# Turning round the order of the states and within-chunk matmuls in a state-space and feed-forward layer

## The chip, the cores and the metric

The kernel runs on one core of one Trainium2 chip. Times are microseconds (us) of device time. The engines are TensorE (PE in the profile; its weight loads are PEld), VectorE (DVE), ScalarE (ACT), GpSimd (POOL) and SyncE (SP, which only issues DMAs here). PE writes into PSUM, of which the kernel uses eight banks; the other engines read the results out of it.

## What is computed

The reference is one layer on x of shape (4, 512, 256): a state-space block and then a feed-forward block, each with a normalization before it and a gate behind it. The state-space block has 32 heads of width 8 with a state of 64:

```python
h = _layernorm(x) * (1 + ca) + sa
proj = h @ W_in.T                                  # xBC, z, A_log
xBC = causal_conv_of_4(xBC) + conv_b               # x, Bm, Cm
a = -softplus(A_log);  Lm = exp(segsum(a))
M = einsum('blhn,bshn,bhls->bhls', Cm, Bm, Lm)
y = einsum('bhls,bshp->blhp', M, x) + D * x
x = x + ga * ((y * silu(z + z_bias)) @ W_out.T)
h = _layernorm(x) * (1 + cb) + sb
x = x + gb * (fwht(silu(h @ W1.T) * (h @ W3.T)) @ W2.T)
```

## The kernel before, in words

The 512 tokens of a batch entry are cut into NC = 8 chunks of Q = 64. Within a chunk, M is formed directly ("products within chunks"). Between chunks, a state is carried: each chunk's own contribution to the state ("states"), a scan over the chunks, and the product of C with the carried state.

The heads are worked on in 8 units n = (half of the heads, batch entry), each of two groups m = 2n and 2n + 1 (pp = m % 2), and each group of four pairs of heads k = 4m + g, g = 0 to 3. So k runs from 0 to 63 and m from 0 to 15. For one k:

- `project` (called twice) makes B and C: six matmuls each (line 251, tiles pbc and pcc, one of three PSUM buffers), then the convolution in `conv`, two instructions on ACT (lines 387 and 389), two on DVE (390, 391), one on POOL (392).
- `prep_l` makes the decays l of that k (PE line 428, tile pl; an exponential on ACT, line 430).
- `attend`, called for every odd k, multiplies C and B chunk by chunk for k - 1 and k into two PSUM tiles pG (line 262). These matmuls have an order written out by hand, in a chain: in each chunk k first, then k - 1. Then DVE multiplies each pG into its l (line 458, one instruction of 128x512 each). That product is what the within-chunk matmuls read.
- `turn_b` transposes B (PE line 464, tile bT) and ACT copies it to SBUF as bt (line 466).

For one group m of four k:

- `states` (line 530): 16 matmuls ps, for t = 0 to 3 (pairs of chunks) and g = 0 to 3, from bt of that g and from xwz of that t. g picks one of four column strips of PE, 32 columns wide. ACT then copies ps out to st (line 535).
- `intra` (line 546): 32 matmuls py, for chunk c = 0 to 7 and g = 0 to 3, from l of that g and from xpad of that chunk, in the same four strips. The two groups of a unit add into the same PSUM tile, so the first matmul of the even group starts the sum.
- `turn_states` (sT, line 557, a scan on DVE in line 559, POOL in 563) and `inter` (pi, line 572) carry the state on.

xpad and xwz are made once per unit, in `x_part3`: for each half hf of the tokens four transposes (line 513), then on DVE one instruction for xpad of chunks 4 hf to 4 hf + 3 (line 517) and two for xwz of t = 2 hf and 2 hf + 1 (line 520). The even group of a unit comes just behind it; the odd group finds both halves long done. bt and l come in the order of k, so those of g = 3 and g = 2 are the latest of a group.

What sets the order: each piece of work has a due time, k plus an offset or 4m + 4 plus an offset, and is traced in the order of these times (an agenda, lines 780 on). A planner of the framework then places the instructions on the five engines: it simulates a timeline and takes, on each engine, the earliest-traced instruction that is ready, and allots PSUM and SBUF buffers on the way. It keeps data dependencies; `issue_after` (the helper `behind` in this kernel) adds an order between two instructions of one engine. In the finished program each engine works its own queue in order. PSUM has three buffers for the projections (tag p), three for everything else of this part (tag m: pl, pG, bT, ps, sT, xt, po) and one each for py and pi.

After the scan, from about 445 us on, the feed-forward block runs (tiles f, pdy, pdyi); its first matmuls are mixed with the last groups of the scan.

Of the kernel before, what the change touches and what calls it, by code (L numbers as in the profile page):

```python
# [17 lines left out]
ALU = mybir.AluOpType  # L18
# [6 lines left out]
NC = S // Q  # L25
# [5 lines left out]
def mamba_ffn(tc, ctx, u, c_t, wmod, win_t, cw, cb, zb, dsk, wo_t, w13_t, w2_t,  # L31
              k_ident, k_reset, k_dl, k_dr, k_had, k_own, out):
    nc = tc.nc
    ve, ac, gp, pe = nc.vector, nc.scalar, nc.gpsimd, nc.tensor
# [25 lines left out]
    def work(shape, name, tag, bufs=2, dtype=F32):  # L60
        return wk.tile(shape, dtype, name=name, tag=tag, bufs=bufs)

    def mtile(shape, name):
        return ps_m.tile(shape, F32, name=name, tag="m")
# [18 lines left out]
    last = {}  # L83

    def behind(*engines):
        stack = ExitStack()
        for e in engines:
            stack.enter_context(tc.issue_after(last[e].ins))
        return stack
# [322 lines left out]
    lts, bcs, ccs, bts, exs, des, xcs, xds, dcs, stt, pys, zts = ({} for _ in range(12))  # L412
# [29 lines left out]
    def attend(k):  # L442


        ks = (k - 1, k)
        pgs = [mtile([128, S], f"pG{n}") for n in ks]
        chain = Chain()
        for c in range(NC):


            for n, pg in list(zip(ks, pgs))[::-1]:
                for j in range(2):
                    i, o = 64 * j, 64 * (j ^ (n % 2))
                    r, l = slice(i, i + 64), slice(Q * c, Q * c + Q)
                    chain.matmul(pg[o : o + 64, l], bcs[n][r, l], ccs[n][r, l], start=True, stop=True,
                                 tile_position=(i, o))
        for n, pg in zip(ks, pgs):
            ve.tensor_tensor(lts[n], pg, lts[n], ALU.mult)  # L458

    def turn_b(k):  # L460
        bc = bcs[k]
# [63 lines left out]
    def states(m):  # L525
        pp = m % 2
        pst = mtile([128, 4, 128], f"ps{m}")
        for t in range(4):
            for g in range(4):
                pe.matmul(pst[32 * g : 32 * g + 32, t], xwz[:, t, 4 * g + 2 * pp : 4 * g + 2 * pp + 2].rearrange("p h q x -> p (h q x)"),  # L530
                          bts[4 * m + g][:, t], start=True, stop=True, tile_position=(0, 32 * g))
        for g in range(4):
            bts.pop(4 * m + g)
        stt[m] = work([128, 4, 128], f"st{m}", "st", 1)
        ac.activation(stt[m], pst, AF.Copy)

    def intra(m):
        n, pp = divmod(m, 2)
        if pp == 0:
            pys[n] = (ps_1.tile([128, S], F32, name=f"py{n}", tag="y"),  # L540
                      ps_1.tile([128, S], F32, name=f"pi{n}", tag="yi"))
        py = pys[n][0]
        for c in range(NC):
            for g in range(4):
                l = slice(Q * c, Q * c + Q)
                pe.matmul(py[32 * g : 32 * g + 32, l], xpad[:, pp, c, g], lts[4 * m + g][:, l],  # L546
                          start=(pp == 0 and c == 0), stop=(pp == 1), skip_group_check=True,
                          tile_position=(0, 32 * g))
        for g in range(4):
            lts.pop(4 * m + g)  # L550
# [229 lines left out]
    for m in range(16):  # L780
        at_time(4 * m + 4 + T["states"], states, m)
        at_time(4 * m + 4 + T["intra"], intra, m)
        at_time(4 * m + 4 + T["turn"], turn_states, m)
        at_time(4 * m + 4 + T["inter"], inter, m)
        if m:
            at_time(4 * m + T["load_d"], load_d, m)
    for k in range(NP):
        if k % 2:
            at_time(k + T["attend"], attend, k)
        at_time(k + T["turn_b"], turn_b, k)  # L790
        if k >= AHEAD:
            at_time(k + T["proj_b"], project, k, 0)
            at_time(k + T["proj_c"], project, k, 1)
        if k >= LOOK_P:
            at_time(k + T["prep_l"], prep_l, k)
# [112 lines left out]
```

## Time and profile before

| | us |
|---|---|
| three runs | 584.75, 587.55, 587.96 (median 587.55) |
| the profiled execution, whole | 587.68 |
| its span, first to last instruction | 585.9 |
| mean granted TensorE clock | 0.988 of full speed |
| PE busy | 549.5 (94%) |
| DVE busy | 401.7 (69%) |
| ACT busy | 387.2 (66%) |
| POOL busy | 325.8 (56%) |

A row of the timeline has the start in us, the length in us (from the first start to the last end of what is merged in the row), the engine, the line, the operation, written and read tiles, a shape and a count; in brackets, the idle time of the engine just before it and what ended it. A matmul of this kernel with two float32 operands shows as two records, so a group of 16 or 32 matmuls shows as 32 or 64. A row of the waits has the waiting instruction, what it waited for, the total in us, how often, and the longest. A row of groups has the count, the busy time and the mean duration of one instruction:

| PE instruction | records | busy us | mean ns |
|---|---|---|---|
| py, L546 | 1024 | 29.9 | 222 |
| ps, L530 | 512 | 22.1 | 275 |
| pG, L262 | 2048 | 40.7 | 222 |
| pi, L572 | 896 | 16.6 | 227 |

The two instructions on DVE that the change orders are 64 of line 458, 683 ns each.

### The profile page before, as it was taken

How to read it: one execution, taken by the hardware profiler on the slowest of the kernel's cores; microseconds unless marked ns; L12 is line 12 of the kernel's file. 1: busy time of each engine (PE TensorE's matmuls, PEld its weight loads, DVE VectorE, ACT ScalarE, POOL GpSimd, SP SyncE). 2: the span in 40 equal slices, each digit the busy share in tenths (PEclk: the TensorE clock that was granted, in tenths of full speed). 3: DMA queues.
4: the chain of work that ended last, by engine and by line, in shares of the span. 5: the costliest groups of instructions: out<-in, count | busy, mean ns of one | idle time of the engine just before them, and what ended most of it. 6: DMA issues, size and time to landing. Idle time of an engine off the chain costs nothing.

```text
span 585.9 us, 16301 instructions
## 1 busy us (share of the span) xinstructions
PE 549.5 (94%) x6867; PEld 432.6 (74%) x6868; DVE 401.7 (69%) x672; ACT 387.2 (66%) x666; POOL 325.8 (56%) x299
## 2 busy tenths in 40 slices
PE   9868899899899989999999899899989999999996
PEld 5545686667687766877777677677767898888886
DVE  5978667977878675889787779787855454333243
ACT  5988779788966877896794787769584242232321
POOL 5862447435635668466465557477666645334341
PEclk9998999999999989999999899999989999999999
DMA  7351101401232343014103142164157037004021
GB/s 230 106 184 35 49 2 74 66 16 59 67 63 56 117 143 121 2 62 137 42 4 113 75 112 104 61 170 149 38 156 286 2 127 217 35 1 152 1 82 36
DMA packets 41793, 51.99 MB, mean 89 GB/s; under 512 B 17943, under 2 KB 29941, under 8 KB 41721
## 3 DMA queue, kind: packets, MB, share of 16 engines
q1 hardware_dynamic: 41448, 50.96, 28.5%
q8 instruction: 54, 0.88, 0.6%
q14 instruction: 19, 0.15, 0.1%
q10 hardware_dynamic: 272, 0.00, 0.0%
HBM read 33.51 MB, written 17.44 MB: 87 GB/s over the span
## 4 chain that ended last, share of the span: by engine, by line
PE 40%; DVE 5%; ACT 4%; POOL 2%; issue 1%; DMA 1%; POOLq 0%; DVEq 0%
PE f L251 15%; PE pcc L251 4%; PE pdy L724 4%; PE pdyi L724 4%; PE pbc L251 3%; PE po L610 2%; PE pG L262 1%; PE py L546 1%; PE bT L464 1%; ACT xn L281 1%; PE ps L530 1%; PE pi L572 1%; DVE cc L390 1%; DVE bc L390 1%; PE pt L291 1%
## 5 line engine op out<-in xcount | busy, mean ns | idle before, releaser
L392 POOL TENSOR_TENSOR bc<-bc,cv 128x509 f32<-128x509 f32 x64 | 69.6, 1088 | 55.8 <-DVE bc L391 37.9
L251 PE MATMUL f<-h,wf 128*128 128x512 f32 x384 | 97.7, 395 | 0.0
L392 POOL TENSOR_TENSOR cc<-cc,cv 128x509 f32<-128x509 f32 x64 | 69.7, 1090 | 50.1 <-DVE cc L391 39.1
L251 PEld LDWEIGHTS f<-h,wf 128*128 128x128 f32 x384 | 69.2, 190 | 12.5
L717 POOL TENSOR_TENSOR fl<-ft,fh 128x512 fp32r<-128x512 f32 x31 | 40.0, 1293 | 57.8 <-ACT fh L716 55.1
L390 DVE SCALAR_TENSOR_TENSOR cc<-pcc,cw_sb,cc 128x511 f32<-128x511 f32 x64 | 47.6, 743 | 32.2 <-ACT cv L389 32.1
L387 ACT ACTIVATE cc<-pcc,cb_sb,cw_sb 128x512 f32<-128x512 f32 x64 | 50.2, 784 | 22.8 <-PE pcc L251 17.3
L251 PE MATMUL pcc<-ht,wq 128*128 128x512 f32 x192 | 55.8, 424 | 6.1 <-DVE bc L391 6.1
L387 ACT ACTIVATE bc<-pbc,cb_sb,cw_sb 128x512 f32<-128x512 f32 x64 | 50.1, 782 | 15.4 <-PE pG L262 14.0
L716 ACT ACTIVATE fh<-ft 128x512 fp32r<-128x512 f32 x32 | 20.2, 631 | 57.6 <-DVE ft L713 27.7
L712 DVE SCALAR_TENSOR_TENSOR ft<-ft,f 128x512 f32<-128x512 f32 x32 | 21.9, 688 | 52.4 <-ACT ft L711 52.3
L251 PE MATMUL pcc<-hr,wq 128*128 128x512 f32 x192 | 54.5, 417 | 2.9 <-DVE bc L391 2.2
L390 DVE SCALAR_TENSOR_TENSOR bc<-pbc,cw_sb,bc 128x511 f32<-128x511 f32 x64 | 47.6, 744 | 11.1 <-ACT cv L389 10.8
L251 PE MATMUL pbc<-hr,wq 128*128 128x512 f32 x192 | 52.4, 406 | 1.4 <-DVE cc L391 1.0
L251 PE MATMUL pbc<-ht,wq 128*128 128x512 f32 x192 | 51.7, 402 | 1.6 <-DVE bc L391 1.6
L251 PEld LDWEIGHTS pcc<-ht,wq 128*128 128x128 f32 x192 | 35.7, 196 | 19.1 <-DVE bc L391 7.0
L391 DVE SCALAR_TENSOR_TENSOR bc<-pbc,cw_sb,bc 128x510 f32<-128x510 f32 x64 | 47.5, 743 | 1.2
L391 DVE SCALAR_TENSOR_TENSOR cc<-pcc,cw_sb,cc 128x510 f32<-128x510 f32 x64 | 47.6, 743 | 1.0
L458 DVE TENSOR_TENSOR l<-pG,l 128x512 f32<-128x512 f32 x64 | 41.2, 683 | 8.3 <-PE pG L262 7.9
L464 PE MATMUL bT<-ident,bc 128*128 128x128 f32 x256 | 41.2, 283 | 4.6 <-ACT bt L466 2.4
L466 ACT ACTIVATE bt<-bT 128x512 f32<-128x512 f32 x64 | 38.8, 606 | 9.8 <-PE bT L464 9.5
L262 PEld LDWEIGHTS pG<-cc,bc 64*64 64x64 f32 x2048 | 34.8, 134 | 13.7 <-issue 9.7
(154 smaller groups left out, 1244.8 us busy)
## 6 DMA issues: line engine op xcount, KB each, us to landing
wq<-win_t SPq DMA_DIRECT2D x16, 256.0 KB
htd<-ht SPq DMA_DIRECT2D x8, 512.0 KB
hr<-htd SPq DMA_DIRECT2D x8, 512.0 KB
h2d<-ht SPq DMA_DIRECT2D x8, 512.0 KB
h<-h2d SPq DMA_DIRECT2D x8, 512.0 KB
x<-u SPq DMA_DIRECT2D x7, 512.0 KB
ex<-pd SPq DMA_DIRECT2D x8, 256.0 KB
ygd<-yg SPq DMA_DIRECT2D x4, 512.0 KB
```

The lines of the kernel that those rows point to most:

```text
L251: last[pe] = pe.matmul(ps, w[:, a, k, c0 : c0 + 128], ht[k][:, b], start=(n == 0), stop=(n == 5))
L262: self.before = pe.matmul(*args, **kw)
L387: ac.activation(dst, ps, AF.Identity, bias=cb_sb[:, tl : tl + 1], scale=w[:, 3:4])
L390: ve.scalar_tensor_tensor(dst[:, 1:], ps[:, : S - 1], w[:, 2:3], dst[:, 1:], ALU.mult, ALU.add)
L391: last["conv"] = ve.scalar_tensor_tensor(dst[:, 2:], ps[:, : S - 2], w[:, 1:2], dst[:, 2:], ALU.mult, ALU.add)
L392: last[gp] = gp.tensor_tensor(dst[:, 3:], dst[:, 3:], v[:, : S - 3], ALU.add)
L458: ve.tensor_tensor(lts[n], pg, lts[n], ALU.mult)
L464: pe.transpose(pt[:, t], bc[:, 128 * t : 128 * t + 128], ident)
L466: ac.activation(bts[k], pt, AF.Copy)
L712: ve.scalar_tensor_tensor(t, t, 1.0, p1, ALU.add, ALU.mult)
L717: (ve if (b, f) == (NB - 1, 7) else gp).tensor_tensor(lo, t, hi.bitcast(F32), ALU.subtract)
L724: last[pe] = pe.matmul(pds[t // 2][:, t % 2], hid[a][:, tok], w2h[f][:, w_], start=(f == 0 and t % 2 == 0 and m == 0), stop=(f == 7 and m ...
```

## The change

In `attend`, DVE's two products were traced in the order k - 1, k, with no order between them; now the one of k is traced first and the one of k - 1 is issued behind it. In `states`, t and g run backwards: t = 3 first, and g = 3 first in each t. In `intra`, the chunks run backwards, c = 7 first, and g in the order 2, 3, 0, 1; the flag that starts the sum moves to the chunk that now comes first. The same matmuls and products are computed.

```diff
-        for n, pg in zip(ks, pgs):
-            ve.tensor_tensor(lts[n], pg, lts[n], ALU.mult)
+        last["l"] = ve.tensor_tensor(lts[k], pgs[1], lts[k], ALU.mult)
+        with behind("l"):
+            ve.tensor_tensor(lts[k - 1], pgs[0], lts[k - 1], ALU.mult)
...
-        for t in range(4):
-            for g in range(4):
+
+        for t in range(4)[::-1]:
+            for g in range(4)[::-1]:
...
-        for c in range(NC):
-            for g in range(4):
+        for c in range(NC)[::-1]:
+            for g in (2, 3, 0, 1):
...
-                          start=(pp == 0 and c == 0), stop=(pp == 1), skip_group_check=True,
+                          start=(pp == 0 and c == NC - 1), stop=(pp == 1), skip_group_check=True,
```

## The prediction

> **What bounds the kernel now.** I read the page's first rows, then the busy time by stage, then TensorE's (PE's) timeline around one pair of groups, then who waited for whom.
>
> ```profile
> span 585.9 us, 16301 instructions
> PE 549.5 (94%) x6867; PEld 432.6 (74%) x6868; DVE 401.7 (69%) x672; ACT 387.2 (66%) x666; POOL 325.8 (56%) x299
> ...
> 60.00:445.00 385.00, 364.57 (x5599) 279.62 (x5594) 297.81 (x484) 298.24 (x514) 230.80 (x212) 0.99 0.28 83
> 445.00:586.00 141.00, 135.96 (x865) 119.76 (x853) 57.15 (x93) 41.83 (x70) 59.67 (x48) 1.00 0.26 85
> ```
>
> The fourth and fifth rows are stretches: length, then busy time of PE, weight loads, DVE (VectorE), ACT, POOL, then the granted clock. From 60 to 445 us, the chunked scan, PE is busy 364.6 of 385.0 us. After that, in the feed-forward stage, PE has no idle until the last microseconds. So whatever PE saves in the scan and does not spend waiting moves the end by as much. About 20 us of PE idle lie in the scan, and they are waits:
>
> ```profile
> PE pcc L251 <- DVE bc L391: 8.4, 14, 2.4
> PE pt L291 <- ACT bt L466: 3.4, 2, 1.7
> ...
> PE ps L530 <- DVE l L458: 0.2, 1, 0.2
> ...
> ACT st L535 <- PE ps L530: 13.9, 8, 4.9
> ```
>
> (total us, times, longest.) The first row: the next projection waits until DVE has read an older one out of PSUM. The third: today PE hardly ever waits at the head of a states group. The last: ACT's queue stands still for a states group that PE has not finished, 13.9 us in 8 places.
>
> The groups that the change reorders look like this. A states group (ps) is 16 matmuls, a within-chunk group (py) 32; each shows as two records, so 32 and 64. Four neighbours work side by side in four column strips.
>
> ```profile
> 260.44 0.65 PE L546 MATMUL py<-l,xpad 128*32 128x64 f32 x32
> 260.92 0.62 PE L530 MATMUL ps<-bt,xwz 128*32 128x128 f32 x16
> 261.46 0.66 PE L464 MATMUL bT<-ident,bc 128*128 128x128 f32 x4
> 262.05 0.54 PE L546 MATMUL py<-l,xpad 128*32 128x64 f32 x24
> 262.41 0.62 PE L530 MATMUL ps<-bt,xwz 128*32 128x128 f32 x16
> 262.85 0.29 PE L546 MATMUL py<-l,xpad 128*32 128x64 f32 x8
> ...
> 269.86 0.31 PE L546 MATMUL py<-l,xpad 128*32 128x64 f32 x4
> 270.10 0.66 PE L464 MATMUL bT<-ident,bc 128*128 128x128 f32 x4
> ```
>
> (start, us, what, count.) The first six rows are an **even group** (m = 8): it is cut in two, since the first half needs only the first half of xpad and xwz, and the rest waits for the second. The last two rows begin an **odd group** (m = 9): two matmuls (4 records, chunk 0 with g = 0 and 1) slip in 12 us before the rest, because their l was ready, and then the group stops at g = 2. Chunks 1 to 7 of g = 0 and 1 had the same l and did not go, so inside one PSUM bank the program keeps the written order. That is what lets a first matmul with the latest operand hold the whole group together.
>
> **The change, part by part.** Nothing is added or removed on PE, and no DMA moves. I price only the order, from starts on PE's timeline ("step": start of the next thing minus start of this one).
>
> *A whole group.* The states group at 312.46 runs in one piece, all 32 records, and the next thing starts at 313.47: 1.01 us. A carry group (pi, the same form as py) has 56 records from 273.68 to 274.60, 0.92 us; eight records more cost 0.11, so py in one piece is 1.03. A lone stretch carries an ending of about 0.14: the states group is 8 rounds of four strips at 0.109 us, or 0.87, and takes 1.01. Both in one stretch share it: 1.01 + 1.03 - 0.14 = 1.90 us.
>
> *Even groups.* Now they take 1.02 + 1.02 = 2.04 at m = 8 and 1.20 + 1.05 = 2.25 at m = 4; all eight, m = 0 to 14: 2.07, 2.24, 2.25, 2.09, 2.04, 2.40, 2.05, 2.29, together 17.4 us, against 8 x 1.90 = 15.2: 2.2 us less. With t and c reversed, the first matmuls need the second half of xwz and xpad, so no first half goes early. But these groups lie where DVE is the later one: the projection before them (258.86) began 0.05 us after DVE freed its buffer (258.81), the one after them (263.11) 0.47 us after. What PE saves there is partly waited away. I take half, **1.1 us**, with 0 and 2.2 as ends.
>
> *Odd groups, main part.* 281.71 to 283.75, 2.04 us, in 14 alternating pieces of ps and py; the eight, m = 1 to 15: 2.03, 2.03, 2.37, 2.03, 2.04, 2.04, 2.04, 2.12, together 16.7 us (without 0.26 idle at 442.9), against 15.2: 1.5 less. The last operands were there before the group began (bt at 279.28, l at 279.62), so nothing on the chip forces the alternation. I take **1.5 us**; 0 if the planner alternates again.
>
> *Odd groups, early piece.* 0.24 us each. At four of the eight (174.67, 269.86, 321.69, 431.96) the next thing follows with no idle, so they are on the path: 4 x 0.24 = **1.0 us**. The other four precede a wait of PE and cost nothing now.
>
> *VectorE's pair.* Each product takes 0.683 us (64 of them) and both are needed. The chain of L262 ends with g odd first, so taking l of k first can begin one round, about 0.11 us, sooner; only 8 waits of DVE are there (7.9 us). The forced order adds no wait for another engine. Since py now begins with g = 2, whose l is then the second product, nothing is late next. I count 0, ends -0.9 and +0.9 (8 x 0.11). A somewhat later st is covered too: at m = 8 st ends at 263.70 and its transposes sT start at 269.11, over 5 us later.
>
> Sum: 1.1 + 1.5 + 1.0 = 3.6 us. The profiled execution took 587.68 us for its span of 585.9; 587.68 - 3.6 = 584.1, and the median of the runs, 587.55, stands 0.1 beside it: **584.0 us**.
>
> [...] In the trace a stretch of 128x32 matmuls costs an ending of about 0.14 us. [...] In the trace PE waited 0.2 us in all at the head of a states group. [...]
>
> **The rivals.**
>
> *A: the group's wait takes the place of the split (slower).* Today the first half of an even group is done while DVE still makes the second. At m = 2 it runs 108.52 to 109.72; DVE ends the second xpad at 111.67 and xwz at 112.34. Take the first half (1.19) away, and the second, which starts at 111.80 now, could start at 110.61, but its first operand comes at 111.67: a hole of 1.06 us. At m = 4 the same reckoning gives 163.38 against 164.00, 0.6; at m = 8 261.03 against 261.32, 0.3: together 2.0 us if the planner finds nothing to put there. Worse, the whole 1.90 us then stands ahead of projections that DVE and ACT wait for. If in all eight even groups the first half (1.02 to 1.20, say 1.1) becomes additional, it is 8 x 1.1 = 8.8 us, less what the odd groups gain and the planner refills, 8.8 - 2.5 = 6.3 at the worst: up to 594. It decides from the point where PE idles over 0.5 us ahead of each even group (8 x 0.5 = 4.0, more than the 3.6). A planner's other order counts here as well: it re-places every later instruction. For it: PE's waits on DVE of up to 2.4 us. Against: at m = 0, 6, 10, 12 and 14 DVE is done before PE comes, and pl, pG and pz stand ready as fill. Half of that, 591, is its middle value.
>
> *B: nothing to be seen.* Where DVE frees PSUM just in time (slack 0.05 to 0.5 us at 210.84, 258.86, 263.11, 296.38, 304.71), PE's gain becomes idle; or the planner, which already had 12 us between early piece and rest, alternates the two groups as before. Then only the early pieces count, 1.0 us or less: 586.6.
>
> *C: more than the sum.* At m = 10, 12 and 14 ACT stood still 4.95, 3.35 and 3.62 us for st, 11.9 of the 13.9, since the second half of ps was placed after 24 output matmuls. A group in one piece also holds one of the three PSUM buffers of tag m for some 2 us instead of 4 (260.92 to 263.70 now; 56.9 to 61.3 at m = 0). If half of the 11.9 is won, 6.0 more: 578.
>
> **How the numbers follow.** A measurement of this kernel tells about 0.5%, 2.9 us, from no change. The forecast, 0.42, spans 581.5 to 586.5; I put 0.27 of it below 584.6 and 0.15 above. C has 0.12 (faster), B 0.14 (same), A 0.32 (slower). Faster 0.27 + 0.12 = 0.39, same 0.15 + 0.14 = 0.29, slower 0.32. The range must reach into A and C, 579 to 593: it leaves out about half of C and the top of A. The likeliest case alone has 581.5 to 586.5.
>
> **What would show it.** In the profile after: ps in rows of 32 and py in rows of 64 or nearly; no x4 row of py; the steps of the 16 groups near 15.2 + 15.2 us in place of 36. A shows as idle of PE put down to ps or py waiting for DVE xwz, xpad or l, or more than 8.4 us at pcc behind DVE. B shows as the same alternating rows, or as fewer us in the groups and as many more idle. C shows as less than 13.9 us of ACT waiting for ps. The forecast is wrong if the groups are whole and PE's idle from 60 to 445 grows by over 2 us.

## The result, and the profile after

The changed kernel takes 593.99 us (median of five runs, 592.36 to 595.25). Five runs of the kernel before beside it gave a median of 584.75. The ratio is 1.0137, 95% interval 1.0100 to 1.0174: **slower by 1.4%**. Forecast were 584.0 and a range of 579 to 593, so both the sign and the range missed. (The forecast counted from 587.55, the median of three of these five runs.) The profiled execution took 595.25 us, its span 593.5, at a mean granted clock of 0.976 (before 0.988).

Of the experiments turned_x and st_dve the profiled execution was disturbed (spans of 611.5 and 2902 us), so no time is read from those two profiles but PE's waits in turned_x's, which ran at a mean granted clock of 0.913 and may show them too small.

In the kernel after, lines behind the edits stand some lines lower: ps is L532, py L548, bT L465, bt L467, xpad L518, xwz L521, st L537, pi L574. In the experiments ps is L531 and st L536 where the blank line of the change is missing.

The page after, span and PE's busy time, and below it the two stretches (length, busy PE, PEld, DVE, ACT, POOL, clock):

```profile
span 593.5 us, 16328 instructions
...
PE 546.8 (92%) x6868; PEld 433.9 (73%) x6868; DVE 401.7 (68%) x672; ACT 386.3 (65%) x666; POOL 325.3 (55%) x299
```

```profile
60.00:445.00 385.00, 354.61 (x5418) 274.92 (x5412) 295.53 (x483) 294.42 (x510) 223.99 (x207) 0.97 0.26 78
445.00:593.50 148.50, 142.85 (x1050) 125.65 (x1042) 60.84 (x98) 45.67 (x76) 66.29 (x54) 0.99 0.28 93
```

PE is busy 2.7 us less than before (546.8 against 549.5) and idle 10.3 us more (593.5 - 546.8 = 46.7 against 585.9 - 549.5 = 36.4). From 60 to 445 us it does 10 us less of its work, which is done later.

The even group m = 8 after, on PE's timeline (start, us, what, count, and in brackets PE's idle ahead of it with its releaser):

```profile
265.33 1.04 PE L514 MATMUL xt<-ident,xd 128*128 128x128 f32 x8
266.13 1.63 PE L251 MATMUL pcc<-hr,wq 128*128 128x512 f32 x6
268.79 1.00 PE L548 MATMUL py<-l,xpad 128*32 128x64 f32 x57 [1.03 <-DVE xpad L518]
269.61 0.28 PE L532 MATMUL ps<-bt,xwz 128*32 128x128 f32 x3
269.63 0.22 PE L548 MATMUL py<-l,xpad 128*32 128x64 f32 x1
269.69 1.04 PE L532 MATMUL ps<-bt,xwz 128*32 128x128 f32 x29
270.48 0.29 PE L548 MATMUL py<-l,xpad 128*32 128x64 f32 x6
270.70 0.66 PE L465 MATMUL bT<-ident,bc 128*128 128x128 f32 x4
```

The group is whole: 64 and 32 records from 268.79, the next thing at 270.70, a step of 1.91 us. Fourteen of the 16 groups are in one piece; at m = 5 three of py's matmuls come later, at m = 10 eleven come 2.1 us earlier. The early row of four records is gone. But PE stands 1.03 us ahead of it. The rows of the waits (total us, times, longest), first three of before that the prediction doesn't show, then those of after:

```profile
DVE l L458 <- PE pG L262: 7.9, 8, 2.7
...
ACT cc L387 <- PE pi L572: 4.8, 7, 1.9
...
PE bT L464 <- ACT bt L466: 2.4, 4, 0.8
```

```profile
DVE l L457 <- PE pG L262: 18.0, 17, 3.7
...
ACT st L537 <- PE ps L532: 13.1, 5, 4.1
...
ACT cc L387 <- PE pi L574: 10.9, 6, 4.0
...
ACT st L537 <- PE py L548: 9.5, 3, 4.7
...
PE py L548 <- DVE xpad L518: 6.6, 4, 2.8
...
PE pcc L251 <- DVE bc L391: 5.8, 9, 2.5
...
PE bT L465 <- ACT bt L467: 4.6, 5, 1.1
...
PE ps L532 <- ACT bt L467: 0.7, 1, 0.7
```

New is the row of py: PE waits 6.6 us at the head of even groups for the second xpad, at m = 0, 2, 4 and 8. With the last row, which is the odd group m = 15, PE's waits at the head of groups are 7.3 us; before they were 0.2. ACT's wait to copy the states out has gone from 13.9 + 0.5 = 14.4 to 13.1 + 9.5 = 22.6 us, nearly all of it at even groups, and its wait for C's buffers (cc), which come free when pi has read them, from 4.8 to 10.9. DVE's wait for the products of C and B (pG) went from 7.9 to 18.0 us.

The longest hole is that of m = 2. Three views of the kernel after: PE, then DVE, then ACT.

```profile
110.77 1.64 PE L251 MATMUL pbc<-ht,wq 128*128 128x512 f32 x6
115.25 1.81 PE L548 MATMUL py<-l,xpad 128*32 128x64 f32 x57 [2.84 <-DVE xpad L518]
...
118.66 0.60 PE L465 MATMUL bT<-ident,bc 128*128 128x128 f32 x4
```

```profile
112.55 0.73 DVE L391 SCALAR_TENSOR_TENSOR cc<-pcc,cw_sb,cc 128x510 f32<-128x510 f32 x1
113.21 0.73 DVE L270 BATCH_NORM_STATS2 bs<-x 128x6 f32<-128x256 f32 x2
113.87 0.72 DVE L390 SCALAR_TENSOR_TENSOR bc<-pbc,cw_sb,bc 128x511 f32<-128x511 f32 x1
114.52 0.67 DVE L518 TENSOR_TENSOR xpad<-xt,own 128x512 f32<-128x512 f32 x1
```

```profile
113.23 0.69 ACT L389 ACTIVATE cv<-pcc,cw_sb 128x512 f32<-128x512 f32 x1
118.63 0.60 ACT L537 ACTIVATE st<-ps 128x512 f32<-128x512 f32 x1 [4.71 <-PE py L548]
```

The planner put the group straight behind pbc. DVE worked without a break, but had three other things ahead of the second xpad. From 112.41 to 115.25 PE stood: bT, pz and pcc are queued behind the group. POOL had written the bc that this bT reads (both of k = 12) by 102.27 us; bT ran at 118.66. ACT's next instruction in order is the copy of this group's states, and it stood 4.71 us. Before, half of this group ran at 108.52 to 109.72, beside work that was ready. In the kernel before, DVE, then PE:

```profile
109.03 0.73 DVE L391 SCALAR_TENSOR_TENSOR cc<-pcc,cw_sb,cc 128x510 f32<-128x510 f32 x1
109.69 0.74 DVE L270 BATCH_NORM_STATS2 bs<-x 128x6 f32<-128x256 f32 x2
110.35 0.73 DVE L390 SCALAR_TENSOR_TENSOR bc<-pbc,cw_sb,bc 128x511 f32<-128x511 f32 x1
111.00 0.67 DVE L517 TENSOR_TENSOR xpad<-xt,own 128x512 f32<-128x512 f32 x1
```

```profile
109.80 1.64 PE L251 MATMUL pbc<-ht,wq 128*128 128x512 f32 x6
111.27 0.60 PE L464 MATMUL bT<-ident,bc 128*128 128x128 f32 x4
111.80 0.58 PE L546 MATMUL py<-l,xpad 128*32 128x64 f32 x26
```

DVE has the same four instructions in the same order. What is new is PE's order: the first half no longer stands ahead of pbc, and bT no longer stands between pbc and the group.

The clock fell too. The same place in stretches of 3.41 us (columns as above):

```profile
107.86:111.27 3.41, 2.90 (x18) 2.48 (x17) 3.38 (x6) 3.33 (x7) 1.09 (x1) 1.00 0.16 39
111.27:114.68 3.41, 1.13 (x5) 0.56 (x3) 3.41 (x9) 2.63 (x5) 1.08 (x1) 1.00 0.12 20
114.68:118.09 3.41, 2.85 (x85) 2.77 (x89) 3.41 (x9) 0.00 (x0) 0.62 (x1) 0.50 0.64 174
118.09:121.50 3.41, 3.41 (x35) 2.92 (x28) 1.67 (x6) 2.42 (x6) 2.53 (x3) 1.00 0.54 88
```

In the second stretch PE is busy 1.13 of 3.41 us; in the third, the granted clock is 0.50. So the group itself took 118.50 - 115.25 = 3.25 us in place of 1.91. Ahead of the end, the profile after has eight stretches of 3.41 us at half clock (two of them in one piece), that of before four.

### The profile page after: what moved, and what is told of

Its sections match the earlier page's. It is cut to its first block, busy times and chain, and to the rows that moved or that the text cites. A ratio compares the mean times of both kernels' runs of the same rounds, so it can differ in the third digit from the quotient of the medians.

```text
span 593.5 us, 16328 instructions
## 1 busy us (share of the span) xinstructions
PE 546.8 (92%) x6868; PEld 433.9 (73%) x6868; DVE 401.7 (68%) x672; ACT 386.3 (65%) x666; POOL 325.3 (55%) x299
## 4 chain that ended last, share of the span: by engine, by line
PE 58%; DVE 17%; ACT 15%; POOL 3%; issue 3%; DMA 3%; SPq 1%; POOLq 0%; ACTq 0%; DVEq 0%
PE f L251 15%; PE pcc L251 8%; PE pbc L251 7%; PE pdy L726 4%; PE pdyi L726 4%; PE pG L262 4%; ACT cv L389 3%; PE py L548 3%; PE bT L465 3%; DVE cc L390 2%; DVE bc L390 2%; PE ps L532 2%; ACT bc L387 2%; DVE bc L391 2%; PE pi L574 2%
## 5 line engine op out<-in xcount | busy, mean ns | idle before, releaser
L251 PE MATMUL pcc<-ht,wq 128*128 128x512 f32 x192 | 53.7, 412 | 6.1 <-DVE bc L391 4.6
L251 PE MATMUL pbc<-ht,wq 128*128 128x512 f32 x192 | 53.4, 414 | 3.0 <-ACT l L430 2.1
L465 PE MATMUL bT<-ident,bc 128*128 128x128 f32 x256 | 41.6, 286 | 7.8 <-ACT bt L467 4.6
L262 PEld LDWEIGHTS pG<-cc,bc 64*64 64x64 f32 x2048 | 34.5, 135 | 14.3 <-issue 11.5
L389 ACT ACTIVATE cv<-pbc,cw_sb 128x512 f32<-128x512 f32 x64 | 44.6, 697 | 0.0
L389 ACT ACTIVATE cv<-pcc,cw_sb 128x512 f32<-128x512 f32 x64 | 44.4, 694 | 0.0
```

The costliest lines, as they stand in the source:

```text
L251: last[pe] = pe.matmul(ps, w[:, a, k, c0 : c0 + 128], ht[k][:, b], start=(n == 0), stop=(n == 5))
L262: self.before = pe.matmul(*args, **kw)
L389: last[ac] = ac.activation(v, ps, AF.Copy, scale=w[:, 0:1])
L465: pe.transpose(pt[:, t], bc[:, 128 * t : 128 * t + 128], ident)
```

## The experiments

Each time is a median, and each ratio is to runs of the kernel before on the same chip, with its 95% interval. All kernels but att_only, odd_only, skip_lo, skip_hi and the controls turn the even groups round, wholly or in part. "Head waits" is the sum of PE's waits at ps and py in the profile.

**The parts alone.** att_only has VectorE's fixed order and the old loops:

```
+        last["l"] = ve.tensor_tensor(lts[k], pgs[1], lts[k], ALU.mult)
+        with behind("l"):
+            ve.tensor_tensor(lts[k - 1], pgs[0], lts[k - 1], ALU.mult)
```

> Only VectorE's two products get their fixed order. The order of the instructions on all engines is that of before, line by line, since k already came first. Both theories: 1.000 within 0.3%; what it shows beyond that is the scatter of the measurement.

585.67 us, 0.9995 (0.9968 to 1.0023). In the program, every engine has the same order as before: the planner already took l of k first. This part is nothing.

odd_only adds the turned loops in odd groups alone (pp = 1):

```
+        for t in (range(4)[::-1] if pp else range(4)):
+            for g in (range(4)[::-1] if pp else range(4)):
...
+        cs = (range(NC)[::-1] if pp else range(NC))
+        for c in cs:
+            for g in ((2, 3, 0, 1) if pp else range(4)):
```

> Only the odd groups (m = 1, 3, ...) are turned round; the even ones, which come just behind xpad and xwz, keep the order of before. Theory H (the hole): the 9 us lost lie at the even groups, which now stand whole at the head of PE's queue and wait there for DVE's second xpad; so this one loses the odd groups' splits alone and comes out 1 to 2.5 us under the kernel before, ratio 0.996 to 0.998. Rival R (another plan): turning any group round makes the planner place everything behind it anew, and it is that which costs; then this one lies some 3 to 5 us above before, about half of the loss.

585.71 us, 0.9978 (0.9955 to 1.0001); head waits 0.7 us. The odd groups are whole (but for three matmuls at m = 5), and at the heads only the 0.7 us of m = 15 have come. They gain 0.2%, by the interval between nothing and 0.45%, where 2.5 us (0.4%) were forecast.

even_only has the two conditions the other way round.

> Only the even groups are turned round. Theory H: the whole loss and a little more, since the odd groups' gain is missing: 594 to 597, with PE's wait for xpad at py at 6 us or more. Rival R: about half of the loss, 588 to 591.

593.01 us, 1.0115 (1.0069 to 1.0162); head waits 6.4 us. The time is just under H's numbers and well over R's. **The whole loss is with the even groups.**

**Which half of the even edit.** even_intra: the odd groups whole, and of the even groups only py turned; even_states: only ps turned.

```
 # even_states, intra: as odd_only; states:
+        for t in range(4)[::-1]:
+            for g in range(4)[::-1]:
```

> Odd groups turned round as in the change; of the even groups only the within-chunk matmuls, while their states keep t = 0 first and so still go in two halves. Theory F: half of the first half's work is moved behind DVE's second xpad, so about half of the even groups' loss: 589 to 591 where the kernel before takes 587. Theory P (plan): the order on ACT and DVE stays nearly that of before, and then the time is that of odd_only, 585 to 587.

588.55 us, 1.0063 (1.0040 to 1.0087); head waits 1.7 us. That is between F and P.

> Odd groups as changed; of the even groups only the states groups are turned round, the within-chunk groups keep the old order. Same computation. Turning the even within-chunk groups alone had cost 588.55 against 585.71 with neither. Theory S (both halves of the edit cost alike, since ACT and PE stand behind either): 588 to 591. Rival X (the cost is PE's wait at py for the second xpad, and the states groups cost nothing because they run behind py): 584.5 to 587, and with the within-chunk groups as the whole cause the sum to 594 would then need the two together.

592.04 us, 1.0100 (1.0062 to 1.0139). This speaks for S, whose range it passes, and against X: the turned states groups alone cost nearly as much as both (1.0137; the two intervals overlap). Its head waits, 2.3 us, are too small for its loss. Its waits:

```profile
ACT st L536 <- PE ps L531: 21.3, 9, 5.0
...
ACT cc L387 <- PE pi L574: 10.7, 7, 3.6
...
PE bT L465 <- ACT bt L467: 6.4, 6, 1.5
...
PE py L548 <- DVE xpad L518: 1.6, 3, 0.9
```

Here the delay shows on ACT (21.3 against 13.9) and, behind it, on PE's wait for bt at the next bT (6.4 against 2.4). That the one brings the other is argued from ACT's order, not tried.

**Is PE's work in the even groups what bounds?** These two leave work out: skip_lo leaves out the first four chunks of py in every even group, skip_hi the last four, with all loops as before. Each has 128 matmuls less.

```
+        for c in range(NC)[0 if pp else NC // 2:]:       # skip_lo
+        for c in range(NC)[:NC if pp else NC // 2]:      # skip_hi
```

> The kernel before, its even groups without the within-chunk matmuls of chunks 0 to 3 (16 of 32 per even group are left out, so part of y is missing). Theory F (free fill): in the kernel before, this first half runs while PE has to wait for DVE in any case; leaving 8 x 0.5 us of it out saves under 1.5 us. Rival (PE bound there as elsewhere): it saves 3 to 4 us, ratio 0.993 to 0.995.

584.36 us, 0.9989 (0.9958 to 1.0019).

> The same with chunks 4 to 7 of the even groups left out instead. Theory F: the second half stands on the path, behind DVE's second xpad, so this saves clearly more than leaving out the first, 3 to 4 us, ratio 0.993 to 0.995. Rival: the same as for chunks 0 to 3.

586.96 us, 1.0033 (1.0015 to 1.0051). So it isn't the second half that lies on the path either. PE is busy some 3 to 5 us less in these profiles (544.4 and 544.5, against 549.5 before and 547.5 in att_only, which has the order of before), and neither is faster beyond its scatter. PE's time at these places is worth little to the end, by skip_lo's interval 2.5 us at most, although PE is busy 94% of the span. Each is also a plan of its own: on ACT, 16 of 666 instructions stand elsewhere than before in skip_lo, 50 in skip_hi.

**The hole taken away by a later due time.** late03 and late09 are the whole change, with the even groups due 0.3 and 0.9 steps later in the agenda:

```
+        late = 0 if m % 2 else 0.3
-        at_time(4 * m + 4 + T["states"], states, m)
-        at_time(4 * m + 4 + T["intra"], intra, m)
+        at_time(4 * m + 4 + T["states"] + late, states, m)
+        at_time(4 * m + 4 + T["intra"] + late, intra, m)
```

> The whole change, but states and intra of the even groups fall due 0.3 later, so that pw and the next transposes bT stand ahead of the even group in PE's queue instead of behind it. Theory H: the fill takes up the hole; PE's wait for xpad at py falls from 6.6 us to under 2, ACT's wait for st from 22.6 us to some 14, and the time to 583 to 588. Rival R: the wait at py falls as well, but the time stays within 3 us of the changed kernel, 591 to 597, because the loss was not there.

595.63 us, 1.0147 (1.0113 to 1.0182). The hole is gone, the loss is not:

```profile
PE bT L465 <- ACT bt L467: 8.2, 7, 1.9
...
PE pG L262 <- issue: 3.7, 1, 3.7
...
PE ps L531 <- DVE l L459: 0.7, 1, 0.7
...
PE py L548 <- DVE xpad L518: 0.6, 2, 0.4
```

By itself this spoke against the hole as the cause. Its control, further down, shows that the later due time costs 1.1% with the old loops as well.

> The whole change with the even groups due 0.9 steps of the planner later, behind work that is ready, so that their last operand is there when PE comes to them. Same computation. Theory W (whole even groups cost where they are put into the plan, through holes): PE's wait at py under 1 us, 585 to 589. Rival D (a whole even group is late for what follows it wherever it stands: ACT's copy, the turned states, the carried states, and then cc's buffers): 591 to 597, with ACT's waits for PE and for cc's buffers larger than in the changed kernel.

588.55 us, 1.0061 (1.0024 to 1.0098), head waits 2.0 us. That is W's range of time, though ACT's wait for C's buffers is 11.4 us, as D has it. No control of this shift was run.

**The clock.** after_warm is the whole change with six matmuls on unused data behind the turned states of m = 0, 2, 4 and 6, where PE in the kernel after stood idle for 1.1 to 2.2 us, at m = 0 and 6 ahead of a stretch at half clock (70.31 and 234.15 us):

```
+        if pp == 0 and n < 4:
+            with behind("sT"):
+                for _ in range(6):
+                    pe.matmul(pys[n][1], idle[:, :128], idle, start=True, stop=True)
```

> The changed kernel plus 24 matmuls of zeros: six of 128x512 bf16 (some 0.2 us each) right behind the transposes sT of the even groups of the first four units, written into pi before its sum begins. The order of everything else is that of the changed kernel. They stand where PE idles some 2 to 2.5 us before the projections that ran at half clock. Theory C (clock): about half of the loss is the half clock that follows PE's new idle; keeping PE busy there raises the mean granted clock from 0.978 to 0.982 or more and brings the time from 594 down by 1 to 4 us, though 5 us of work are added. Rival: the half clock only falls where PE waits anyway; then the added work leaves the time where it is or puts 1 to 5 us on top, 594 to 599.

594.02 us, 1.0151 (1.0122 to 1.0180). The mean granted clock of the timed runs rose from 0.978 to 0.982, but 24 added matmuls cost some 5 us of PE, an estimate from a row of the kernel after in which eight of this form take 1.89 us (the last of them 0.38):

```profile
9.02 1.89 PE L97 MATMUL warm<-idle 128*128 128x512 bf16 x8
```

It decides nothing.

**ACT's place.** st_dve is the whole change with the copy of the even groups' states on VectorE:

```
+        if pp:
             ac.activation(stt[m], pst, AF.Copy)
+        else:
+            ve.tensor_copy(stt[m], pst)
```

> The whole change, with the copy of an even group's states out of PSUM on VectorE in the place of ACT. Same computation. Theory A (ACT standing 0.9 to 4.7 us at the copy of each even group, 10 us in sum more than before, holds up conv, bt and cc and is the larger part of the loss): ACT's wait for ps falls to some 12 us, all in odd groups, and the time to 587 to 590. Rival (the loss is PE's hole at py and the half clock after it): the hole stays at 6 us, VectorE takes 8 x 0.6 = 5 us more, and the time stays at 592 to 596.

594.34 us, 1.0136 (1.0091 to 1.0181). Theory A falls in this form: taking the copy out of ACT's queue wins nothing. Whether VectorE now stood in its place can't be read, as said above.

**Beginning with the half that is ready first, with the same loops.** turned_x is the whole change, and `x_part2` and `x_part3` make the second half first, so that the turned loops begin with what is ready first:

```
-        for hf in range(2):
+        for hf in (1, 0):
...
-        for hf, xd in enumerate(xds.pop(n)):
+        for hf, xd in xds.pop(n):
```

> The whole change, and x's two halves made in the other order too (second half of xd, xpad and xwz first), so that the turned-round even groups begin again with the half that is ready first, and are cut in two again. Same computation. Theory L (what costs is that an even group begins with its last operand: everything behind it waits for that): even groups split, PE's wait at py for xpad under 1.5 us in sum, ACT's wait for st of even groups back near 2, time as with the odd groups alone, 583.5 to 587. Rival P (the turned loops only draw another order from the planner, and some draws are bad): anything from 583 to 596 with split groups; over 590 would speak for P and against L.

586.66 us, 1.0005 (0.9978 to 1.0033). The loops, the odd groups and the order of VectorE's two products are those of the change; the even groups are cut in two again, and the loss is gone. **What costs is that an even group begins with its last operand.** Turning the loops round costs nothing by itself. The planner's order goes with it, though: on DVE, ACT and POOL turned_x has the order of odd_only, tile for tile, while in the kernel after 33 of DVE's 672, 40 of ACT's 666 and 7 of POOL's 299 instructions stand elsewhere. So turned_x takes back the wait and the new plan together, and doesn't tell what each costs.

**C's buffers.** cc9 is the whole change with nine buffers for C, b_cc9 the control with the loops of before. The first of the places that change:

```
-        dct, nm, nb = ((bcs, "bc", 3), (ccs, "cc", 8))[half]
+        dct, nm, nb = ((bcs, "bc", 3), (ccs, "cc", 9))[half]
```

> The whole change, with nine buffers for C (cc) in the place of eight. Same computation. Theory B (a whole even states group is copied, turned and carried later, so C's buffers come free later: ACT's wait for the carried group pi before it writes cc rose from 4.8 to 11 us in every kernel with whole even states groups, and attend and its products come late by as much): that wait falls under 5 us and the time to 587 to 590. Rival L (what PE loses is lost at the group itself, where everything behind the last operand waits): the wait for pi falls, the time stays at 592 to 595.

594.84 us, 1.0164 (1.0136 to 1.0192); no row of ACT waiting for pi is left, head waits 5.9 us. (The 11 us "in every kernel" are not so: even_only has 7.5 us of this wait, after_warm 7.0.)

> Control: the loops of before (with VectorE's fixed order, which had moved nothing) and nine buffers for C. Same computation. By theory B 584 to 586.5, as ACT's wait for pi was 4.8 us and mostly covered; by its stronger form 582 to 584; by the rival no change from before, 584.5 to 588.

586.79 us, 1.0030 (1.0009 to 1.0050), head waits 0.8. Theory B falls: ACT no longer waits for C's buffers, and nothing is won.

**The last operand made earlier.** x_early4 and x_early7 are the whole change with x's spread copies and transposes due earlier; b_early7 has the loops of before:

```
-        x2=3.46, x3=3.77
+        x2=2.76, x3=3.07        # x_early7; x_early4: 3.06, 3.37
```

> The whole change, with x's spread copies and their turn (the operands that are ready last) due 0.4 steps of the planner earlier, about 2.5 us. Same computation. Theory L (an even group that begins with its last operand is late by that operand, and so is all behind it): PE's wait at py for xpad falls from 6.6 under 2 us, ACT's at the even copies from 9.1 towards 5, and the time to 586 to 590. Rival P (the turned loops draw a worse order of the other work, whatever the operand does): 591 to 596 with the waits gone.

591.05 us, 1.0096 (1.0058 to 1.0134). That is the lower end of P's range, but the waits at py have not gone (head waits 6.5 us), so it doesn't tell the two apart.

> As x_early4, with 0.7 steps, about 4.5 us. Theory L: the even groups find their operands ready and the time falls to that of the odd groups alone, 583.5 to 587. Rival P: over 590.

599.00 us, 1.0230 (1.0194 to 1.0265), the slowest of all. P's number came, and L's did not. The profile shows what L had missed: xpad is early now, but l and bt have become the last operands, and the turned groups begin with those of g = 2 and 3:

```profile
PE ps L531 <- ACT bt L467: 4.6, 4, 1.3
PE po L612 <- DMA yr<-ygd: 4.5, 1, 4.5
...
PE py L548 <- DVE l L459: 3.6, 5, 2.7
```

The head waits are 8.2 us.

> Control for x_early7 (599.0): the loops of before, with VectorE's fixed order, and the same 0.7 steps earlier for x. Same computation. If whole even groups lose by themselves, this stays near before, 584 to 589. If the earlier x draws the bad order whatever the loops are, 594 to 600, and x_early7 says nothing on the turned loops.

589.35 us, 1.0047 (1.0020 to 1.0075), head waits 3.3 us. The same shift with the old loops costs 0.5%, with the turned ones 2.3%. Not all of the difference need lie at the groups: PE also waits 4.5 us for a DMA at po in x_early7 (second row above) and 1.9 us in b_early7.

> Control for late03 (595.6): the loops of before, with VectorE's fixed order, and the even groups due 0.3 steps later. Same computation. If whole even groups lose by themselves also where no hole stands ahead of them, this stays near before, 584 to 588. If the later due time costs by itself, 592 to 596, and late03 doesn't speak against the hole as the cause.

591.75 us, 1.0108 (1.0067 to 1.0149), head waits 1.0 us. The later due time costs by itself.

Kernels that differ in the order of the loops alone, or (first row) in which half of x is ready first, stand in pairs; in the last two rows only one of the two loops of the even groups is turned:

| last operand first / ready operand first | head waits, us | ratio of the two |
|---|---|---|
| after / turned_x | 7.3 / 0.7 | 1.013 (1.009 to 1.018) |
| x_early7 / b_early7 | 8.2 / 3.3 | 1.018 (1.014 to 1.023) |
| cc9 / b_cc9 | 5.9 / 0.8 | 1.013 (1.010 to 1.017) |
| late03 / b_late03 | 1.8 / 1.0 | 1.004 (0.998 to 1.009) |
| even_states / odd_only | 2.3 / 0.7 | 1.012 (1.008 to 1.017) |
| even_intra / odd_only | 1.7 / 0.7 | 1.009 (1.005 to 1.012) |

(Each ratio is the quotient of the two ratios to before, its interval from the root of the sum of the squared half widths.) Where a whole group makes PE wait 5 us more, the kernel is 1.3 to 1.8% slower than its partner; in late03, where it waits 0.8 us more, the two can't be told apart. The last two rows don't go with the waits: 1.6 and 1.0 us more at the heads, and 1.2 and 0.9% (7 and 5 us) slower. So PE's waits at the heads are not the whole price.

## Why the prediction was wrong, step by step

*A whole group, 1.90 us*: right. The groups in one piece take 1.91 to 1.93 us, only that of m = 2, at half clock, 3.25.

*VectorE's pair, 0*: right, in every instruction's order.

*Odd groups, 1.5 + 1.0*: the groups came together as forecast. The gain is 0.2%, 1.3 us, about half; its interval, 0 to 2.6, has room for the 2.5 and for nothing. Whether the premise of the next step was at fault here too isn't shown.

*Even groups, "I take half, 1.1 us"*: **this is the step that failed**, and with it the wait at the head of these groups, which the sum put at nothing. In place of 1.1 us won, the even groups alone cost 1.15%, some 6.8 us (even_only); in place of no wait at their heads there were 6.6 us. The step rests on the first part's sentence that whatever PE saves in the scan and does not spend waiting moves the end by as much, and it took the waiting as half of the saving. skip_lo and skip_hi speak against that sentence: some 3 to 5 us of PE's work left out there made the kernel 0.1% faster in the one, 0.6 us, by its interval 2.5 us at most, and no faster in the other. As far as they show, the first half of an even group had run in time that PE would mostly have waited anyway. Joining it to the second half moved it from a place that was nearly free to one where DVE, ACT and the next projections wait.

*The waits and rival A.* A had the place and the mechanism; its operands and tiles are those of the row `PE py L548 <- DVE xpad L518`. The holes were reckoned as 1.06, 0.6 and 0.3 us at m = 2, 4 and 8, with the starts and DVE's ends of the trace before. Measured were 2.84, 2.4 and 1.03, and 0.3 at m = 0. That reckoning kept the old times around the group, whereas PE's order changed: at m = 2 it came to the group straight behind pbc, and bT, 0.53 us, no longer stood between the two. DVE's order there is that of before; PE was 1.1 us further ahead of it (its pcc began 5.58 us before the second xpad, in the kernel before 4.50). A named the planner's other order, and set no price on it. The point it gave, PE idle over 0.5 us ahead of each even group, was passed on the average: 6.6 us are 0.8 for each of eight, though four of them had no hole. A's top, 594, came out by luck: its sum for that was 8.8 us of added work of PE, and PE's busy time fell.

*PE's order.* In the kernel after, PE worked on nothing behind the group while the group waited: in the 2.84 us of m = 2, bT stood behind it, and its operand had been written by 102.27 us. The sum had no term for such a wait, though rival A had reckoned 2.0 us of holes. The 0.2 us that PE waited at the head of a states group before came from a program in which no group began with its last operand.

*The clock*, no term of the sum. Taking the timed runs of these kernels together, each against its kernel's mean, the time rises by 0.67 us (standard error 0.04) for each us of clock lost, (1 - clock) x time. After lost 13.2 us on average, before 6.1 to 7.4 on its chips, so some 6.4 x 0.67 = 4.3 us of the difference of about 8 go with the clock. Nearly as much, some 3.5 us, is left at equal clock. That is an estimate, and it doesn't say which of clock and waiting brings the other.

The account of the two profiles closes in another way: by their steps, without the idle behind the early pieces, the groups take 3.9 us less of PE (32.7 against 36.6, with m = 2 at half clock). So the saving of PE's time that the forecast counted, 3.6 us, did come. Stretches at half clock elsewhere and the rest add 1.2, so PE is busy 2.7 less; it is idle 10.3 us more, 7.1 of that at the heads of groups. 10.3 - 2.7 = 7.6 us is the longer span.

*Signs that were named.* Groups whole: yes. "PE's idle from 60 to 445 grows by over 2 us" as proof of error: it grew by 10.0. A's "more than 8.4 us at pcc behind DVE": no, 5.8; the wait had moved to py. C: ACT waited more for the states, not less; of the 11.9 us at m = 10, 12 and 14 that C hoped to win, 11.2 are still there. C had read these three places wrongly: in the kernel before, too, ps stood there in one piece (32 records at 312.46, for one), and only py was split.

**What stays open.** That the loss comes from beginning with the last operand is shown (turned_x and the pairs). How it divides between PE's wait at the head, the copy that stands in an in-order queue behind it, the planner's new order and the clock is open: even_states loses nearly as much with 2.3 us of head waits, st_dve shows that ACT's queue isn't decisive, cc9 that C's buffers aren't, and no kernel has the new order without the late operand. And a plan costs by itself: kernels with the old loops range from 0.9995 to 1.0108 by a shifted due time or one more buffer alone, so that no single kernel of this list proves more than its partner allows.

## What to carry to other kernels

Before an order is changed so that a group starts with its latest operand, ask what the early part of that group was filling. A split that uses idle time costs the engine busy time and the kernel next to nothing: here half of py's matmuls in every even group, left out, gave 0.1% (skip_lo, 0.9958 to 1.0019). An in-order queue with a group at its head that waits holds everything behind it, on this engine and on those that wait to read the group: at m = 2 PE stood 2.84 us and ACT 4.71. And an engine busy 94% is not thereby the bound: leave out a piece of its work at the place in question and see whether the end moves.

## What the runs showed of the hardware

**Stretches at half clock, and how busy PE was ahead of them.** In the profiles of before and after the granted clock is 1.0 or 0.5. In 18 profiles (all but turned_x's and st_dve's) the stretches at half clock ahead of the end last 3.41 us or twice that, and in each profile their starts lie whole multiples of 3.413 us apart: in before they start at 52.88, 209.89, 325.95 and 435.17 us, in after at 32.76, 43.00, 70.31 (6.83 us long), 114.68, 234.15, 387.75 and 442.36. The grid lies elsewhere from profile to profile: counted from the span's start, the starts of before are 1.68 us behind a multiple of 3.413, those of after 2.04. I cut the profiles into such windows, from 19 us on. Behind a window in which PE was busy less than 44%, the next was at half clock in 44 of 45 cases; behind 44 to 60% in 31 of 91; above 60% in 8 of 2833. In the profiles of before and after alone these are 4 of 4, 7 of 14 and 1 of 313. In even_states, PE's timeline:

```profile
67.01 1.64 PE L251 MATMUL pbc<-ht,wq 128*128 128x512 f32 x6
...
70.83 0.63 PE L465 MATMUL bT<-ident,bc 128*128 128x128 f32 x4 [1.52 <-ACT bt L467]
72.24 0.38 PE L428 MATMUL pl<-dr,dl 94*128 94x512 bf16 x1 [0.79 <-DVE sn L561]
72.88 2.47 PE L251 MATMUL pcc<-ht,wq 128*128 128x512 f32 x6 [0.27 <-DVE bc L391]
```

Three gaps of 1.52, 0.79 and 0.27 us, of the first only the last 0.77 us, make the window from 70.06 to 73.47 busy 1.59 us (47%). From 73.47 to 76.88 the granted clock is 0.50, and six matmuls take 2.47 us against 1.64. Whether a given hole costs this may then depend on the execution, if the grid lies elsewhere in each execution of one kernel too. That is an estimate from the two grids above; late09's runs, from 586.4 to 594.6 us with clocks of 0.991 to 0.977, fit it.

**A wait for nothing that the profile shows.** In late03 PE stood 3.71 us in one piece (row `PE pG L262 <- issue`), in the kernel after 1.14 us at nearly the same place in the work. Its cause was not tried.
